# Transposing the second batch's quantised x as pairs of bytes, and loading its ctx with neighbouring rows in a partition

## The chip, the cores and the metric

The kernel runs on one core of one Trainium2 chip. The metric is the time of one execution on the device in microseconds. Before the change it is 1090.87 us, the median of three runs that lie between 1089.13 and 1091.78 us.

## The reference

There are two batches, each with an x of 1024 x 2048 and a ctx of 2048 x 2048, in float32. Two layers follow each other, and each adds to x.

```python
def fake_quant(x, scale, zp):
    q = jnp.clip(jnp.round(x / s + z), 0.0, 255.0)
    return (q - z) * s
...
x = x + jnp.matmul(fake_quant(_layernorm(x)), fake_quant(ctx_4096))
z = _layernorm(x)
x = x + z @ kernel + bias + lora_of_the_group(z) + shared_lora(z)
```

The first layer normalises each row of x, rounds it to whole numbers from 0 to 255, rounds ctx in the same way, and multiplies the two. The second layer multiplies a normalised x with a 2048 x 2048 matrix and adds low-rank terms. Its eight groups of 256 rows have gates of their own.

## The kernel before

The work is cut by batch (b = 0, 1), by group of 256 rows (g = 0 to 3, two tiles of 128 rows each, so a tile has an index m = 0 to 7), and by block of 512 columns (n = 0 to 3).

**x.** A tile's preparation is the class `XTile`. `stats`, `variance`, `root` and `factors` find the mean and the scale (VectorE, but for one square root on ScalarE). `row` writes the 2048 rounded values as bytes into `q8` (in the second batch ScalarE, line 409). `centre` subtracts 128 and writes bfloat16 into `qh`, one half of 1024 columns at a time, and its accumulator gives half of the row's sum (ScalarE, line 412). `turn` transposes that half in eight blocks of 128 x 128 on TensorE into a PSUM tile `pt` (line 423). `place` copies `pt` into the bfloat16 tile `c1T`, with the features on the partitions (line 428, VectorE; for some tiles of the first batch line 427, ScalarE). `total` turns the two half sums into `r_s`, the correction for the zero point (line 432).

**ctx.** Each load from memory (line 213, SyncE's queue) brings 256 rows of 512 columns into one of ten buffers `lit`. `round_ctx` rounds them on ScalarE to int16 (line 458); that frees the buffer, and the next load of the queue can be issued. `centre_ctx` clips and centres them on VectorE into `c2` (line 464). `column_term` sums a block's columns (lines 486 to 511).

**The product.** A `Pair` is one group times one column block: two tiles j, for each of which `begin` (line 526, ScalarE, high priority) writes the corrections into PSUM, and 16 matmuls of 512 columns add to them (line 530). `end` adds the result to `y` (line 547, VectorE), and line 551 takes statistics for the second layer.

**The second layer** is a block matrix product of seven outer steps by seven inner ones (line 829, float32). During the last outer step of the first batch, `meanwhile` already prepares the second batch: after inner step s it rounds two pieces of ctx, and after steps 1 to 4 it prepares the tiles m = 0 to 3. Tiles 4 to 7 are prepared later, between the second batch's products, once `opened`, the first of them, is done.

**What sets the order.** The first batch's first layer follows an order written out by hand (`STEPS`). Everything else is put in order at build time by a list scheduler, which takes for each engine the ready instruction of highest priority, and priority is the order in the program. At run time every engine and every DMA queue works in that fixed order. SyncE's queue holds the loads of ctx, of x (line 226) and of the weights; ScalarE's queue also issues the stores of the finished output (line 855). The x of the second batch goes into the same `y` tiles that hold the first batch's result, so a load of x has to wait for a store; the second halves of the rows of tiles 4 to 7 come last.

Of the kernel before, what the change touches and what calls it, by code (L numbers as in the profile page):

```python
# [11 lines left out]
BF16 = mybir.dt.bfloat16  # L12
U8 = mybir.dt.uint8
I16 = mybir.dt.int16
AF = mybir.ActivationFunctionType
# [5 lines left out]
P = 128  # L21
# [77 lines left out]
def tile_quant_xattn_then_lora_ffn(  # L99
# [17 lines left out]
    nc = tc.nc  # L117
    B, S, D = x.shape
    KT = D // P
    MT = S // P  # L120
    NB = 512
# [9 lines left out]
    KH = KT // 2  # L131
# [8 lines left out]
    ps_m = ctx.enter_context(tc.tile_pool(name="ps_m", bufs=2, space=PSUM))  # L140
# [17 lines left out]
    r_s = const.tile([P, MT], F32, tag="r_s", name="r_s")  # L158
# [13 lines left out]
    def flat(t):  # L172
        return t.rearrange("p k n -> p (k n)")
# [3 lines left out]
    lb = lora_bt.rearrange("(n c r) i -> n c r i", n=NL, c=NC)  # L177

    def raw_src(b, n, r):
        return [ctx_in[b, ds(2 * r * P, 2 * P), ds(n * NB, NB)].rearrange("(k p) n -> p k n", p=P)]  # L180

    def ad_src(t, n, h):

# [4 lines left out]
    for b in range(B):  # L188
        for n in range(2):
            todo.extend((b, raw_src(b, n, r)) for r in range(KT // 2))  # L190
        if b == 0:
            todo.extend((b, m) for m in range(4, MT))
        for n in range(2, 4):
            for r in range(KT // 2):
                todo.append((b, raw_src(b, n, r)))
                if r in ((3, 7) if n == 2 else (5, 7)):
                    todo.extend((b, ad_src(la, 2 * (n - 2) + r // 6 if n == 3 else r // 4, h)) for h in range(2))
        for n in range(NN):
            todo.extend((b, ad_src(lb, n, h)) for h in range(2))
# [79 lines left out]
    s12, d1, d2, kdd = (k_s[:, i : i + 1] for i in range(4))  # L279
    n_centre = const.tile([P, 1], F32, tag="n_centre", name="n_centre")  # L280
# [17 lines left out]
    ident_h = const.tile([P, P], BF16, tag="ident_h", name="ident_h")  # L298
# [67 lines left out]
    class XTile:  # L366


        def __init__(self, b, m, c1T, wk):
            self.b, self.m, self.nm = b, m, f"{b}_{m}"  # L370
            self.on_vector = b == 0 and m not in ROWS_ON_SCALAR
            g, tok = m // MG, ds((m % MG) * P, P)
            self.y = y[g][:, m % MG, :]

            wf = flat(wk)
            self.q8 = wf[:, ds((m % 2) * (D // 4), D // 4)].bitcast(U8)
            self.qh = wf[:, D // 2 : D].bitcast(BF16)
            self.to = [c1T[g][:, ds(h * KH, KH), tok] for h in range(2)]
            self.pt = [None, None]

# [44 lines left out]
        def place(self, h):  # L425
            if self.b == 0 and h == 1 and self.m in PLACED_BY_SCALAR:
                return nc.scalar.copy(self.to[h], self.pt[h])
            return nc.vector.tensor_copy(self.to[h], self.pt[h])  # L428

        def total(self):  # L430

            nc.vector.tensor_scalar(
                r_s[:, self.m : self.m + 1], self.rsum[:, 0:1], self.rsum[:, 1:2], d2, ALU.add, ALU.mult
            )

    def prep_x(b, m, c1T, wk):

        x = XTile(b, m, c1T, wk)
        x.stats(*range(NN))
        with tc.high_priority() if b == 0 else nullcontext():  # L440
            x.variance()
            x.root()
            x.factors()
            x.row()
        for h in range(2):
            x.centre(h)
            x.turn(h)
            x.place(h)
        x.total()

    def quantise(c2, r):
# [569 lines left out]
    for b in range(B):  # L1021
        if b == 0:
            open_c2(0)
            open_c2(1)
            with in_order(mybir.EngineType.DVE, mybir.EngineType.Activation, mybir.EngineType.PE):
                opened, begun = entry()
            next_block(1)
            with tc.issue_after(last_of[mybir.EngineType.DVE]):
                for p in begun.values():
                    p.stats()  # L1030
        else:
            gate_matrix(b)
            opened = xattn_pair(b, 0, 0, c1T, c2[0])
            xattn_pair(b, 0, 1, c1T, c2[0])
            for g in range(2):
                xattn_pair(b, 1, g, c1T, c2[1])
            for g in range(2, GPB):
                for m in range(g * MG, (g + 1) * MG):
                    with tc.issue_after(opened.ins):
                        prep_x(b, m, c1T, wk)  # L1040
                for n in range(2):
                    xattn_pair(b, n, g, c1T, c2[n])
                    if g + 1 == GPB:
                        next_block(n)
                        if n == 0:
                            for r in range(NR):
                                quantise(c2[2], r)
                                if r % 4 == 3:
                                    lora_a_step(b, r // 4)
                            column_term(b, 2, c2[2])  # L1050
# [64 lines left out]
        def meanwhile(o, s):  # L1115
# [27 lines left out]
            if 1 <= s <= 4:  # L1143
                prep_x(nb, s - 1, state["c1T"], state["wk"])
# [77 lines left out]
```

## Time and profile before

| | |
|---|---|
| runs | 1089.13, 1090.87, 1091.78 us |
| span of the profiled execution, first to last instruction | 1086.6 us |
| median less that span | 4.3 us |
| TensorE matmul, busy | 1063.4 us, 98% |
| VectorE, busy | 759.3 us, 70% |
| ScalarE, busy | 247.6 us, 23% |
| DMA, mean rate | 241 GB/s |
| second batch: `row` / `centre` / `place` / transposes | 8 / 16 / 16 / 128 instructions |

A busy share is the union of an engine's instructions over the span. The end of a matmul is modelled, so a busy TensorE need not be one at its peak rate. Times are counted from the start of the span, and no time of the execution that was profiled is given beside its span. The passage that the change touches runs from about 505 us (the last outer step of the first batch's second layer) to about 626 us (the second batch's third column block).

### The profile page before, as it was taken

The page shows a single profiled execution, that of the slowest core. Times are in us where ns is not written, and L with a number is a line of the kernel's source. Part 1 is how long each engine was busy: PE and PEld are TensorE (multiplying, and loading weights), DVE is VectorE, ACT ScalarE, POOL GpSimd, SP SyncE. Part 2 cuts the span into 40 slices and gives each one's busy share as a digit, 9 for nine tenths or more (in the row PEclk, how much of TensorE's full clock was granted, in tenths as well). Part 3 has the DMA queues.
Part 4 walks back from the last instruction along what each step waited for, and adds up shares of the span by engine and source line. Part 5 has one row for each costly group of instructions (what it writes and reads, how often), then busy time and mean ns, then how long its engine had stood idle before and what let it go on. Part 6 is the DMA issues. An engine that isn't in the chain of part 4 may idle for free.

```text
span 1086.6 us, 10640 instructions
## 1 busy us (share of the span) xinstructions
PE 1063.4 (98%) x3932; PEld 491.3 (45%) x3932; DVE 759.3 (70%) x941; ACT 247.6 (23%) x351; POOL 267.8 (25%) x112
## 2 busy tenths in 40 slices
PE   5999999999999999999999999999999999999998
PEld 2444445544444444444444433555444444444443
DVE  7986776756877686677858645757569677756851
ACT  5866133210000000001676631331000000000000
POOL 0000003243434314362000000034344532253500
PEclk7999999999999999999999999999999999999999
DMA  9979758876897575798682394679668874748511
GB/s 344 378 200 295 214 189 327 311 250 218 290 361 271 181 269 182 255 357 300 221 281 49 124 245 164 222 273 349 237 237 292 293 266 154 270 144 301 212 40 58
DMA packets 120380, 261.35 MB, mean 241 GB/s; under 512 B 11400, under 2 KB 15624, under 8 KB 119304
## 3 DMA queue, kind: packets, MB, share of 16 engines
q1 hardware_dynamic: 99840, 219.24, 59.1%
q10 hardware_dynamic: 20168, 40.38, 10.9%
q0 software_dynamic: 320, 1.05, 0.3%
q8 instruction: 31, 0.51, 0.2%
q14 instruction: 21, 0.17, 0.1%
HBM read 224.99 MB, written 37.75 MB: 242 GB/s over the span
## 4 chain that ended last, share of the span: by engine, by line
PE 87%; DVE 5%; DMA 4%; ACT 2%; issue 1%; SPq 0%; ACTq 0%
PE fu L829 34%; PE fv L829 17%; PE pa L530 14%; PE fw L829 9%; DMA lit<-in_ctx_dram 3%; PE pl L695 3%; PE px L649 3%; PE ptz L633 2%; DMA y<-in_x_dram 1%; PE pg_b L576 1%; DVE st L383 1%; PE pg_a L576 1%; ACT big L412 1%; PE pt L423 1%; DVE big L629 1%
## 5 line engine op out<-in xcount | busy, mean ns | idle before, releaser
L829 PE MATMUL fu<-big,lit 128*128 128x512 f32 x896 | 395.3, 593 | 0.0
L829 PEld LDWEIGHTS fu<-big,lit 128*128 128x128 f32 x896 | 168.7, 190 | 206.2 <-issue 204.9
L530 PE MATMUL pa<-big,big 128*128 128x512 bf16 x1024 | 238.8, 381 | 5.0 <-DVE big L428 2.6
L829 PE MATMUL fv<-big,lit 128*128 128x512 f32 x448 | 197.9, 594 | 0.0
L772 POOL TENSOR_TENSOR lit<-lit,lit 128x1024 f32<-128x1024 f32 x56 | 164.2, 2940 | 116.4 <-PE fw L829 49.2
L763 POOL TENSOR_TENSOR lit<-lit,lit 128x1024 f32<-128x1024 f32 x40 | 100.2, 2508 | 289.1 <-DMA lit<-zs 257.7
L772 DVE TENSOR_TENSOR big<-big,big 128x2048 f32<-128x2048 f32 x56 | 159.6, 2853 | 5.9 <-PE ptz L633 5.3
L530 PEld LDWEIGHTS <-big 128*128 128x128 bf16 x1024 | 96.7, 98 | 136.5 <-issue 31.8
L853 DVE TENSOR_TENSOR y<-y,fu 128x1024 f32<-128x1024 f32 x92 | 108.6, 1215 | 50.7 <-PE fu L829 50.5
L829 PEld LDWEIGHTS fv<-big,lit 128*128 128x128 f32 x448 | 84.3, 190 | 105.0 <-issue 104.7
L853 DVE TENSOR_TENSOR y<-y,fv 128x1024 f32<-128x1024 f32 x48 | 56.8, 1218 | 89.4 <-PE fv L829 89.4
L458 ACT ACTIVATE q2b<-lit,sc,inv 128x1024 int16<-128x1024 f32 x64 | 76.3, 1232 | 161.8 <-DMA lit<-in_ctx_dram 126.1
L763 DVE TENSOR_TENSOR big<-big,big 128x2048 f32<-128x2048 f32 x40 | 104.2, 2604 | 11.8 <-DMA big<-in_w_dram 11.8
L829 PE MATMUL fw<-big,lit 128*128 128x512 f32 x224 | 99.6, 593 | 0.0
L680 POOL DMA_DIRECT2D bp<-bd x4 | 2.7, 664 | 376.8 <-DVE rstd_z L358 183.4
L684 ACT COPY pl<-bias 128x1024 f32<-128x1024 f32 x16 | 16.3, 1018 | 294.4 <-DVE y L706 281.4
L547 DVE SCALAR_TENSOR_TENSOR y<-pa,k_s,y 128x1024 f32<-128x1024 f32 x32 | 41.0, 1280 | 47.0 <-PE pa L530 46.8
L829 PEld LDWEIGHTS fw<-big,lit 128*128 128x128 f32 x224 | 41.8, 190 | 51.4 <-issue 50.2
L853 DVE TENSOR_TENSOR y<-y,fw 128x1024 f32<-128x1024 f32 x24 | 28.4, 1216 | 50.9 <-PE fw L829 50.9
L526 ACT ACTIVATE pa<-bp,r_s 128x512 f32<-128x512 f32 x58 | 39.0, 685 | 84.8 <-PE pa L530 54.8
L383 DVE BATCH_NORM_STATS2 st<-y 128x6 f32<-128x512 f32 x64 | 41.4, 680 | 5.4 <-DMA y<-in_x_dram 5.3
L551 DVE BATCH_NORM_STATS2 st<-y 128x6 f32<-128x512 f32 x64 | 40.1, 678 | 0.1
(92 smaller groups left out, 637.3 us busy)
## 6 DMA issues: line engine op xcount, KB each, us to landing
big<-in_w_dram SPq DMA_DIRECT2D x96, 1024.0 KB
lit<-zs SPq DMA_DIRECT2D x88, 512.0 KB
lit<-in_ctx_dram SPq DMA_DIRECT2D x64, 512.0 KB
out_dram<-y ACTq DMA_DIRECT2D x30, 512.0 KB
zs<-lit ACTq DMA_DIRECT2D x24, 512.0 KB
lit<-in_lora_a_dram SPq DMA_DIRECT2D x32, 256.0 KB
lit<-in_lora_bt_dram SPq DMA_DIRECT2D x32, 256.0 KB
y<-in_x_dram SPq DMA_DIRECT2D x16, 512.0 KB
```

Of the source, the lines that this page charges most:

```text
L383: nc.vector.bn_stats(st1[:, self.m, n, :], self.y[:, ds(n * NB, NB)])
L458: nc.scalar.activation(qi, t, AF.Relu, bias=z2, scale=inv2)
L526: nc.scalar.activation(self.pa[:, j, :], colt[self.n], AF.Identity, bias=r_s[:, m : m + 1])
L530: nc.tensor.matmul(self.pa[:, j, :], self.c1T[:, k, ds(j * P, P)], self.c2[k // 8][:, k % 8, :], start=not self.begun[j], stop=(k == KT - ...
L547: return nc.vector.scalar_tensor_tensor(yp, self.pa, s12, yp, ALU.mult, ALU.add)
L551: nc.vector.bn_stats(st2[:, self.g * MG + j, self.n, :], y[self.g][:, j, ds(self.n * NB, NB)])
L649: nc.tensor.matmul(px[i * 2 * R : (i + 1) * 2 * R, :], acat[:, k, ds(3 * pr + i, 2), :].rearrange("p s r -> p (s r)"), zqs[i][k // KQ][:, ...
L695: nc.tensor.matmul(pl[j][i][:, half], axT[rows, pr, ds(j * P, P)], bt[rows, half], start=False, stop=True, skip_group_check=True,)
L763: line(eng.tensor_tensor(got[0], got[0], got[1], ALU.add if terms[1][2] > 0 else ALU.subtract))
L772: line(eng.tensor_tensor(out_t, at[p], at[q], op))
L829: nc.tensor.matmul(ps[m], at[:, k, ds(m * P, P)], bt[:, k, :], start=(opens and k == 0), stop=(ends and k == KQ - 1), skip_group_check=True,)
L853: line(nc.vector.tensor_tensor(yp, yp, whole[chain], op))
```

## The change

For the second batch a tile's bytes are not centred before the transposes. `turn_pairs` reads two neighbouring bytes as one bfloat16 value and transposes the row in eight blocks in place of sixteen. A partition of the PSUM tile then holds two neighbouring features, one in each byte. `place_pairs` reads the bytes out of PSUM with a step of two, subtracts 128 and writes the bfloat16 tiles, in two ScalarE instructions of 1024 elements. `sum_row` runs once more over the 2048 bytes on ScalarE, for the row's sum alone; what else it writes to `qh` is not read. `total` multiplies that one sum. Since features 2p and 2p+1 of each 256 now stand in partition p, the ctx of the second batch is loaded so that rows 2p and 2p+1 stand in partition p. The first batch is untouched.

```diff
     def raw_src(b, n, r):
-        return [ctx_in[b, ds(2 * r * P, 2 * P), ds(n * NB, NB)].rearrange("(k p) n -> p k n", p=P)]
+        rows = "(k p) n -> p k n" if b == 0 else "(p k) n -> p k n"
+        return [ctx_in[b, ds(2 * r * P, 2 * P), ds(n * NB, NB)].rearrange(rows, p=P)]
...
             self.qh = wf[:, D // 2 : D].bitcast(BF16)
+            self.qh2 = self.qh
...
+        def turn_pairs(self):
+
+            self.pairs = ps_m.tile([P, KT // 2, P], BF16, tag="pm", name=f"pq_{self.nm}")
+            two = self.q8.bitcast(BF16)
+            for r in range(KT // 2):
+                nc.tensor.transpose(self.pairs[:, r, :], two[:, ds(r * P, P)], ident_h)
+
+        def place_pairs(self):
+            bytes_of = self.pairs.rearrange("p r t -> p (r t)").bitcast(U8).rearrange("p (r t e) -> p r e t", e=2, t=P)
+            for h in range(2):
+                nc.scalar.activation(
+                    self.to[h].rearrange("p (r e) t -> p r e t", e=2),
+                    bytes_of[:, ds(h * KH // 2, KH // 2)],
+                    AF.Identity,
+                    bias=n_centre,
+                )
+
+        def sum_row(self):
+
+            nc.scalar.activation(self.qh2, self.q8, AF.Identity, bias=n_centre, accum_out=self.rsum[:, 0:1])
+
         def total(self):
 
+            if self.b:
+                nc.vector.tensor_mul(r_s[:, self.m : self.m + 1], self.rsum[:, 0:1], d2)
+                return
             nc.vector.tensor_scalar(
...
-        for h in range(2):
-            x.centre(h)
-            x.turn(h)
-            x.place(h)
+        x.turn_pairs()
+        x.place_pairs()
+        x.sum_row()
         x.total()
```

## The prediction

> **What bounds the kernel now.** I began with the page's first part and its costliest groups.
>
> ```profile
> PE 1063.4 (98%) x3932; PEld 491.3 (45%) x3932; DVE 759.3 (70%) x941; ACT 247.6 (23%) x351; POOL 267.8 (25%) x112
> ...
> L530 PE MATMUL pa<-big,big 128*128 128x512 bf16 x1024 | 238.8, 381 | 5.0 <-DVE big L428 2.6
> ```
>
> TensorE is busy for 98% of the span, and that is real work: in the chain 16 matmuls of line 530 take 3.56 us, 222 ns each, back to back. A TensorE instruction that disappears is therefore worth its full time, unless the instructions behind it are not ready either. ScalarE's 23% says little, because it is a mean over stages. So I asked for the second batch's preparation by stages. The columns are the stretch in us, its length, the busy us of PE, its weight loads, DVE, ACT and POOL with their counts, then the granted clock, the DMA share and GB/s.
>
> ```profile
> 541.90:564.00 22.10, 21.98 (x119) 9.31 (x118) 10.65 (x27) 19.97 (x22) 0.00 (x0) 1.00 0.77 240
> 564.00:579.80 15.80, 15.80 (x72) 6.95 (x71) 13.91 (x32) 4.24 (x8) 0.00 (x0) 1.00 0.77 231
> 579.80:609.80 30.00, 28.92 (x177) 14.03 (x175) 20.90 (x49) 22.69 (x30) 0.00 (x0) 1.00 0.00 1
> ```
>
> In the first stretch (tiles 2 and 3, and ctx of the second column block) ScalarE has 2.1 us left of 22.1, in the third (tiles 4 to 7) it works 22.7 us of 30, and in between, 4.2 of 15.8. The ordered chain of waits over this passage shows what ends last:
>
> ```profile
> 560.26 1.23 ACT q2b L458
> 561.51 0.44 DVE big L464
> ...
> 561.98 8.89 DMA y<-in_x_dram
> ...
> 579.79 2.10 ACT big L409
> ...
> 584.34 0.62 PE pt L423 x8
> ...
> 595.75 2.08 ACT big L409
> 597.83 2.26 ACT big L412 x4
> 600.09 0.62 ACT pa L526
> ...
> 600.75 3.61 PE pa L530 x16
> ```
>
> Read downwards: a rounding of ctx on ScalarE ends at 561.49 and frees a buffer; the ctx load that waited for it is issued; behind that load in SyncE's queue stand the last two x loads, which go out at 561.98 and land 8.9 us later; VectorE then needs 8.9 us for statistics and factors (it is busy for 13.9 of these 15.8 us), and tile 4's `row` starts at 579.79. From there ScalarE sets the pace. Yet TensorE has nearly always something to do: it idles 1.03 us between 580 and 590, and 4 us in the whole of 500 to 720. So this passage stands on an edge: TensorE is full, and ScalarE is late by hardly anything.
>
> The prices are in the groups by shape (out <- in, count | busy us, mean ns), first of 505 to 705 us, then ScalarE's of the whole span, for a copy that the first batch makes:
>
> ```profile
> L412 ACT ACTIVATE big<-big,n_centre 128x1024 bf16<-128x1024 uint8 x16 | 18.2, 1137 | 1.6 <-PE pt L423 1.5
> L409 ACT ACTIVATE big<-y,ox,kx 128x2048 uint8<-128x2048 f32 x8 | 16.6, 2084 | 2.8 <-DVE ox L402 2.8
> ...
> L428 DVE COPY big<-pt 128x1024 bf16<-128x1024 bf16 x16 | 10.5, 681 | 0.1
> ...
> L423 PE MATMUL pt<-ident_h,big 128*128 128x128 bf16 x128 | 9.5, 219 | 2.1 <-ACT big L412 2.1
> ```
>
> ```profile
> L427 ACT COPY big<-pt 128x1024 bf16<-128x1024 bf16 x6 | 6.0, 1005 | 0.8 <-PE pt L423 0.8
> ```
>
> **The change part by part.**
>
> TensorE: 64 of 128 transposes go. Eight in a row take 0.45 us in the chain, so 64 are 3.6 us, 1.8 of them during the second layer (tiles 0 to 3) and 1.8 between the products (tiles 4 to 7). All of it lies on a full TensorE. Its waits for `centre`, 2.1 us in all (1.09 at 528, twice 0.51 at 583 and 584), become one wait per tile for `row`. Between nothing and 2.1 us is won there; I take 1.0, the two at tile 4, since the wait at 528 is a difference between planned and real time that can come back elsewhere.
>
> VectorE: 16 copies of 0.68 us go, 10.9 us. Only where VectorE is on the path would that count, and in the stretch from 564 to 579.8, where it is, there is no copy. I take nothing for it. `total` is one [128 x 1] operation as before.
>
> ScalarE, per tile. Before: `row` and two `centre`, 4.4 us from one tile's start to its end (548.49 to 552.98). After: `row` 2.08; `sum_row`, 2048 bytes: from the rows of 1024 and 2048 elements each further element costs 0.93 ns, so 1.14 + 0.95 = 2.09, plus 0.1 for reading the accumulator; and two unpackings. No row of the trace reads bytes with a step of two out of PSUM. The nearest are line 427 (same size, out of PSUM, 1.005) and line 412 (bytes, with the bias, 1.137). I take 1.1, less the 0.09 by which neighbours overlap; if a stepped byte counted as two elements it would be 2.08, the far end. Together 6.3 us, 1.9 more per tile and 15 us over eight.
>
> [...]
>
> The added wait: an unpacking stands in ScalarE's queue and waits for transposes, where VectorE's copy did. Behind it are the next `row`, the ctx roundings (line 458), `begin` (line 526) and the output stores (line 855). `sum_row` needs only `row`; a list scheduler will most likely put it into that gap, ahead of the unpacking. A tile is then ready 1.9 us later, and `begin`, which needs the sum, hardly later.
>
> ScalarE's 1.9 us by stage. Tiles 0 and 1 (525 to 541): 3.8 us, which the idle 5.0 us before 541.87 hides; without that gap they would add to the next. Tiles 2 and 3: 3.8 us against 2.1 us of idle, and work that starts at most 1.8 us sooner as the second layer ends sooner. So the sixth rounding of ctx, which lets the x loads out, comes between 1.8 us sooner and 3.8 us later; I take 1.0 later, for the idle time lies in four pieces and not all can be used. The x loads, VectorE's 8.9 us and tile 4's `row` follow: 580.8.
>
> Tiles 4 to 7, from the start of `row` 4: before, tile 5's products started 13.1 us later (592.9), tile 7's 30.0 us later (609.8). After: two tiles of 6.3 and three `begin` of 0.62 give 14.5, less half an unpacking, as the first eight matmuls need only that: about 14. Tile 7: four tiles and eight `begin`, 25.2 + 5.0 = 30.2. TensorE has two pairs between the two, 14.2 us, with 0.9 of transposes and 1.0 of loaded products (line 576), and does not take longer. So the 1.8 us of transposes saved here and the 1.0 of waiting are spent on ScalarE. Those two matmuls of line 576, at 608.8 before, may then stand behind tile 7's start and not in a wait: nothing to 1.0, I take 1.0.
>
> ctx rows: the loads keep 256 pieces of 2 KB; only their order changes. The trace has no such load. Mixed stretches with other layouts ran at 335 to 369 GB/s (558 to 570), so I allow 5% either way, 0.5 us on a landing of 9.7, and take nothing; ten buffers loaded ahead hide it, and without them half a microsecond would reach the third block.
>
> Sum: 1.0 later at tile 4, 0.2 in its pace, 1.0 behind it: +2.2 us. From there to the end all is bound to the products' end (the buffers of the third block are those of the first), so it stays. Against the profiled span of 1086.6 that gives 1088.8. What lies around the span is 4.3 us, median less span, so the forecast is 1093.1; its own range, by the bounds above, is 1090 to 1096.5.
>
> **The rivals.** *ScalarE is hidden, and TensorE's saving counts.* If the ctx roundings or the x loads are put ahead of tile 3's sum and unpacking, `row` 4 starts with the second layer's end, 1.8 us sooner or more, and the 3.6 us of transposes and the 2.1 us of waits are won: 1090.9 - 5.7 = 1085.2. For it: VectorE is lighter, and ScalarE idles 11.6 us of 15.8 just before tile 4. Against it: 19.97 of 22.10 busy before. It decides at a tile 4 that starts before 578.
>
> *ScalarE's queue holds the x loads.* Everything of tiles 2 and 3 plus a wait for transposes inside ScalarE's queue (each up to 1.1 us, as at 528) stands ahead of the store at 555.23 or of the sixth rounding: 3.8 + 2 x 1.1 = 6.0 later, and 1.2 behind it: +7.2, 1098.1. For it: the chain above runs through that rounding, and three queues pass it on. Against it: VectorE and SyncE each have slack there. It decides from 3 us of delay at the last x loads.
>
> *Bytes out of PSUM cost double.* 16 x 1.0 us more on ScalarE, 4.0 of it in tiles 4 to 7 and 2.0 to 4.0 before: +9, about 1100. The only sign is that no row shows the form.
>
> **How the numbers follow.** What a measurement of this kernel can tell from no change is about 0.3%, 3.3 us. The forecast (ScalarE spends what TensorE saves) gets 0.52: 0.31 of it within 0.3%, 0.21 slower, as its range passes 1094.1. The hidden ScalarE gets 0.24, of which 0.22 faster and 0.02 within. The held x loads get 0.17 and the double bytes 0.07, of which 0.01 within and 0.23 slower. So 0.22 faster, 0.34 the same, 0.44 slower. The range of 8 in 10 reaches to the first rival's 1085 and nearly to the last one's: 1085.0 to 1099.5.
>
> **What would show it.** Right: line 423 gone from the second batch but for 64 transposes of 0.056 us; unpackings of 1.0 to 1.15 us, `sum_row` of 2.1; ScalarE's busy time up by 15 us; `row` 4 near 581; TensorE's idle time up by some 3 us between 575 and 612, waiting for line 526 or for the unpacking. Wrong: `row` 4 before 578 or after 584; an unpacking beyond 1.3 us; a time that comes or goes before 505 or after 630; or roundings and x loads in another order around the second layer's end, since that order is the scheduler's and I could only guess it.

## The result, and the profile after

The changed kernel takes 1093.36 us (median; 1090.43 to 1098.56), the kernel before 1088.52 beside it (1086.89 to 1091.78). The ratio is 1.0046, with a 95% interval of 1.003 to 1.0062: slower by about 4.8 us, and by more than the 0.3% that a measurement can tell from no change. The forecast was 1093.1.

The profiled execution has a span of 1094.9 us, 8.3 above that of before. 3.5 of these come late, from a wait for weights: their load is issued at 718 us, VectorE makes an operand of them, TensorE's `fw` (line 854, 829 before) waits 2.08 us for it, and its first ten matmuls then take 6.25 us in place of 4.50, at a granted clock of 0.50. The first line is of the changed kernel, the second of the one before:

```profile
730.22 6.25 PE L854 MATMUL fw<-big,lit 128*128 128x512 f32 x10 [2.08 <-DVE big L788]
```

```profile
723.40 4.50 PE L829 MATMUL fw<-big,lit 128*128 128x512 f32 x10
```

Kernels with the old orders show the same wait in some profiles (`rows_only`, `before_begin_first` below) and kernels with the new ones do not show it in others, so I leave it out; the readings below stop at the first `px` matmul of the second batch (line 674; 705.00 us before, 709.82 after: 4.82 us apart). How often this wait comes in either kernel is not known, and so its share of the 4.8 us is not known either. It is hardly all of them, for the fastest executions of the two kernels are 3.5 us apart as well.

In the changed kernel `row` is line 411, the transposes 437, the unpacking 442, the row sum 451, the ctx rounding 483, `begin` 551, the products 555. First the page (busy us, share, count), then the groups by shape of 505 to 712 us:

```profile
PE 1064.4 (97%) x3868; PEld 489.5 (45%) x3868; DVE 752.0 (69%) x925; ACT 261.0 (24%) x351; POOL 263.8 (24%) x112
...
L555 PE MATMUL pa<-big,big 128*128 128x512 bf16 x1024 | 241.3, 385 | 11.1 <-ACT pa L551 7.3
```

```profile
L442 ACT ACTIVATE big<-pq,n_centre 128x1024 bf16<-128x1024 uint8 x16 | 16.9, 1102 | 2.4 <-PE pq L437 2.4
...
L451 ACT ACTIVATE big<-big,n_centre 128x2048 bf16<-128x2048 uint8 x8 | 16.0, 1998 | 0.0
...
L451 ACT ACTIVATION_READ_ACCUMULATOR big<-big,n_centre 128x1 f32 x8 | 1.5, 191 | 0.0
```

An unpacking takes 1.102 us and a row sum 1.998: the two prices that no row of before showed. ScalarE has 13.4 us more to do. The products' idle time has gone from 5.0 to 11.1 us, 7.3 of it released by `begin`. The third stage, in the columns used before the change, and two stretches of 2 us:

```profile
579.80:609.80 30.00, 25.96 (x130) 11.85 (x129) 14.20 (x39) 28.16 (x28) 0.00 (x0) 0.89 0.00 1
...
584.00:586.00 2.00, 1.08 (x3) 0.40 (x3) 1.33 (x9) 2.00 (x5) 0.00 (x0) 0.50 0.00 0
586.00:588.00 2.00, 2.00 (x6) 0.73 (x5) 0.00 (x0) 2.00 (x3) 0.00 (x0) 0.50 0.00 0
```

In the third stage TensorE is busy 2.96 us less than the 28.92 of before, and ScalarE works 28.2 us of 30. The granted clock, 1.00 in all three stages before, is 0.89; it is 0.50 from 584 to 591, as the short stretches begin to show. TensorE's timeline (start, us; in brackets the idle time before the first of a group, and what ended it) and the ordered chain:

```profile
582.22 0.62 PE L437 MATMUL pq<-ident_h,big 128*128 128x128 bf16 x8 [0.69 <-ACT big L411]
584.92 8.23 PE L555 MATMUL pa<-big,big 128*128 128x512 bf16 x24 [2.08 <-ACT pa L551]
...
593.43 5.34 PE L555 MATMUL pa<-big,big 128*128 128x512 bf16 x24
```

```profile
565.50 8.37 DMA y<-in_x_dram
...
580.07 2.10 ACT big L411
...
582.19 2.09 ACT big L451 x2
584.29 0.59 ACT pa L551
...
584.92 8.23 PE pa L555 x24
```

TensorE's products stop at 581.53, eight transposes follow tile 4's `row`, and then it waits for a `begin` that stands in ScalarE's queue behind tile 4's `row` and row sum. That `begin`, the second of block 1, group 1, runs at 584.20 in both kernels, and the products go on at 584.92 in both. TensorE's timeline before:

```profile
584.34 0.62 PE L423 MATMUL pt<-ident_h,big 128*128 128x128 bf16 x8 [0.51 <-ACT big L412]
584.92 4.48 PE L530 MATMUL pa<-big,big 128*128 128x512 bf16 x20
```

Only, the products now stop 1.2 us sooner (581.53 against 582.70), and 8 transposes in place of 16 fill the time. TensorE stands still for 3.39 us but for these, and then 24 matmuls take 8.23 us; the next 24 take 5.34.

One more wait came that the profile of before does not have. ScalarE's timeline in the third block:

```profile
634.37 1.24 ACT L483 ACTIVATE q2b<-lit,sc,inv 128x1024 int16<-128x1024 f32 x1 [2.14 <-DMA lit<-in_ctx_dram]
635.52 0.67 ACT L551 ACTIVATE pa<-bp,r_s 128x512 f32<-128x512 f32 x1
```

A rounding waits for its ctx load, and the `begin` behind it lets TensorE wait 2.33 us at 636.24. TensorE's timeline, two lines of the changed kernel and one of before:

```profile
622.86 0.38 PE L555 MATMUL pa<-big,big 128*128 128x512 bf16 x1 [0.78 <-ACT pa L551]
...
636.24 4.04 PE L555 MATMUL pa<-big,big 128*128 128x512 bf16 x18 [2.33 <-ACT pa L551]
```

```profile
620.29 0.38 PE L530 MATMUL pa<-big,big 128*128 128x512 bf16 x1 [0.78 <-ACT pa L526]
```

At the first matmul of the second block's last tile the changed kernel is 2.57 us behind (622.86 against 620.29); at `px`, behind this wait, it is 4.82.

### The profile page after: what moved, and what is told of

It reads as the page before. It is cut to its first block, busy times and chain, and to the rows that moved or that the text cites. A ratio compares the mean times of both kernels' runs of the same rounds, so it can differ in the third digit from the quotient of the medians.

```text
span 1094.9 us, 10488 instructions
## 1 busy us (share of the span) xinstructions
PE 1064.4 (97%) x3868; PEld 489.5 (45%) x3868; DVE 752.0 (69%) x925; ACT 261.0 (24%) x351; POOL 263.8 (24%) x112
## 4 chain that ended last, share of the span: by engine, by line
PE 86%; DMA 5%; DVE 5%; ACT 2%; issue 1%; SPq 0%; ACTq 0%; DVEq 0%
PE fu L854 33%; PE fv L854 17%; PE pa L555 15%; PE fw L854 9%; PE pl L720 3%; PE px L674 3%; PE ptz L658 2%; DMA lit<-in_ctx_dram 2%; DMA lit<-in_lora_a_dram 1%; PE pg_b L601 1%; DMA y<-in_x_dram 1%; PE pg_a L601 1%; DVE st L385 1%; DMA big<-in_w_dram 1%; ACT big L451 1%
## 5 line engine op out<-in xcount | busy, mean ns | idle before, releaser
L555 PE MATMUL pa<-big,big 128*128 128x512 bf16 x1024 | 241.3, 385 | 11.1 <-ACT pa L551 7.3
L797 POOL TENSOR_TENSOR lit<-lit,lit 128x1024 f32<-128x1024 f32 x56 | 162.1, 2903 | 119.2 <-PE fw L854 46.9
L788 POOL TENSOR_TENSOR lit<-lit,lit 128x1024 f32<-128x1024 f32 x40 | 98.1, 2454 | 294.2 <-DMA lit<-zs 255.0
L797 DVE TENSOR_TENSOR big<-big,big 128x2048 f32<-128x2048 f32 x56 | 163.0, 2914 | 5.9 <-PE ptz L658 5.3
L788 DVE TENSOR_TENSOR big<-big,big 128x2048 f32<-128x2048 f32 x40 | 105.5, 2637 | 12.9 <-DMA big<-in_w_dram 12.9
L385 DVE BATCH_NORM_STATS2 st<-y 128x6 f32<-128x512 f32 x64 | 41.3, 682 | 6.5 <-DMA y<-in_x_dram 6.4
L489 DVE TENSOR_SCALAR big<-q2b 128x1024 bf16<-128x1024 int16 x64 | 27.6, 440 | 21.4 <-ACT q2b L483 18.4
```

What stands on the lines that cost most here:

```text
L385: nc.vector.bn_stats(st1[:, self.m, n, :], self.y[:, ds(n * NB, NB)])
L489: nc.vector.tensor_scalar(c2[r // 4][:, ds(2 * (r % 4), 2), :], qi, QMAX, CENTRE, ALU.min, ALU.subtract)
L555: nc.tensor.matmul(self.pa[:, j, :], self.c1T[:, k, ds(j * P, P)], self.c2[k // 8][:, k % 8, :], start=not self.begun[j], stop=(k == KT - ...
L788: line(eng.tensor_tensor(got[0], got[0], got[1], ALU.add if terms[1][2] > 0 else ALU.subtract))
L797: line(eng.tensor_tensor(out_t, at[p], at[q], op))
```

## The experiments

Theory A: the loss arises at tile 4, from the gap before 585 us and the clock behind it. Theory B: it is ScalarE's pace. Where an expectation means something else by a letter, it says so. "px" is the first `px` matmul against the 705.00 us of before.

| kernel | row 4 | gap before 586, transposes in it | clock behind | px | ratio to before, interval |
|---|---|---|---|---|---|
| changed | 580.07 | 3.39, 8 | 0.50 | +4.82 | 1.0046, 1.003 to 1.0062 |
| rows_only | 579.27 | | 1.00 | +0.60 | 1.0008, 0.9996 to 1.0019 |
| early_tiles | 581.18 | 4.30, 8 | 0.50 | +3.93 | 1.0023, 1.0009 to 1.0037 |
| late_tiles | 580.47 | 2.98, 8 | 0.50 | +1.68 | 1.0023, 1.0003 to 1.0043 |
| fill_gap | 579.39 | filled | 1.00 | +0.64 | 1.001, 1.0 to 1.0021 |
| after_begin_first | 582.35 | 3.95, 16 (at 590) | 1.00 | -0.27 | 1.0007, 0.999 to 1.0023 |
| before_begin_first | 584.39 | 5.50, 32 (at 594) | 1.00 | +4.82 | 1.0041, 1.0023 to 1.0058 |
| begin_mid | 579.02 | 2.97, 8 (at 589) | 0.50 | +0.85 | 1.0004, 0.9991 to 1.0017 |
| sum_vector | 579.44 | | 1.00 | -0.11 | 0.999, 0.9971 to 1.001 |
| sum_in_row | 576.74 | | 1.00 | -3.47 | 0.998, 0.996 to 0.9999 |
| fill_transposes | 579.81 | 3.47, 31 | 1.00 | +3.23 | 1.0043, 1.0025 to 1.0061 |
| after_third | 579.87 | 3.15, 8 | 1.00 | +0.54 | 1.0026, 1.0008 to 1.0044 |
| fill_transposes_third | 580.67 | 3.28, 31 | 1.00 | +2.12 | 1.0015, 0.9999 to 1.003 |

The gap is the time from the end of one product to the start of the next. px comes from one profiled execution each, the ratio from repeated runs; the two need not agree.

**rows_only**: the kernel before with the loads' row order alone.

```diff
-        return [ctx_in[b, ds(2 * r * P, 2 * P), ds(n * NB, NB)].rearrange("(k p) n -> p k n", p=P)]
+        rows = "(k p) n -> p k n" if b == 0 else "(p k) n -> p k n"
+        return [ctx_in[b, ds(2 * r * P, 2 * P), ds(n * NB, NB)].rearrange(rows, p=P)]
```

> The kernel before with the new row order of the second batch's ctx loads alone; its contraction then meets rows of ctx in another order than features of x. Every engine's and queue's order is that of before, so it isolates the loads. Theory A (ScalarE's added work makes begin and the tiles late, and a gap in TensorE's work lowers its clock): no difference, within 0.1% of before; the landing times of the ctx loads as before. Rival B (the loads themselves are slower, and the third column block waits for them): most of the 4.8 us, 2 to 5 us slower than before, with waits for ctx between 620 and 640 us.

1089.36 against 1088.32 us: no difference that can be told, so the loads' order is not where the loss is.

**early_tiles and late_tiles**: the new path for tiles 0 to 3 alone (m < 4), and for tiles 4 to 7 alone (m >= 4).

```diff
-        x.turn_pairs()
-        x.place_pairs()
-        x.sum_row()
+        if m < 4:
+            x.turn_pairs()
+            x.place_pairs()
+            x.sum_row()
+        else:
+            for h in range(2):
+                x.centre(h)
+                x.turn(h)
+                x.place(h)
```

(`total` takes its branch by the same condition.)

> The changed kernel with tiles 4 to 7 prepared in the old way (their features then don't meet the rows of ctx that belong to them). Theory A: tiles 0 to 3 are prepared under the second layer, where ScalarE has room; they save 1.8 us of transposes, and the gap before 585 us does not grow much: 0 to 2 us faster than before. Rival B (loads) or a rival C (ScalarE's work on tiles 2 and 3 holds back the x loads): 2 to 5 us slower than before, row 4 later than 581.

> The changed kernel with tiles 0 to 3 prepared in the old way (their features then don't meet the rows of ctx that belong to them). Theory A: the loss is here, 3 to 6 us slower than before, with a granted clock of 0.5 for some us around 585 and waits for begin behind a row sum. Rival C: no slower than before, as ScalarE's queue around the second layer's end is that of before.

1091.6 and 1090.09 against 1088.32 us. Each half loses by itself, and neither is the one that gains. Both expectations of theory A missed: the early tiles came as rival C had it (3.3 us slower, the x loads out at 566.22, `row` 4 at 581.18), and the late ones lost 1.8 us, with the halved clock, in place of 3 to 6. With the early tiles alone TensorE reaches tile 4 sooner, and the time goes into a longer wait, before the first transposes:

```profile
584.60 0.62 PE L425 MATMUL pt<-ident_h,big 128*128 128x128 bf16 x8 [3.72 <-ACT big L414]
```

**fill_gap**: nine idle matmuls behind tile 4's transposes, seven of which fall into the gap; all other orders as in the changed kernel (`last` is the last of those transposes).

```diff
...
+            if self.m == 4:
+                with tc.issue_after(last.ins):
+                    junk = ps_m.tile([P, NB], F32, tag="pm", name=f"junk_{self.nm}")
+                    for _ in range(9):
+                        nc.tensor.matmul(junk, zeros_h, ones_h[:, 0:1].to_broadcast([P, NB]), start=True, stop=True)
```

> The changed kernel with nine matmuls of 512 columns into an unused PSUM tile, put behind tile 4's transposes; all else stays in its order, and seven of the nine fall into TensorE's 2.08 us wait before 584.92. Theory A with the clock: the granted clock stays at 1.0 after that wait, the 24 matmuls that took 8.23 us take 5.3, and the kernel is 2 to 3 us faster than the changed one, some 1 to 3 us slower than before, although it does more work. Without the clock (the gap is only a wait for begin): the same as the changed kernel, or slower by up to the 0.4 us of the two matmuls that fall elsewhere.

1090.48 against 1088.32 us, though TensorE does more work. Its timeline and its third stage:

```profile
582.00 1.69 PE L442 MATMUL junk<-ones_h,zeros_h 128*128 128x512 bf16 x7
584.24 3.61 PE L560 MATMUL pa<-big,big 128*128 128x512 bf16 x16 [0.56 <-ACT pa L556]
```

```profile
579.80:609.80 30.00, 27.35 (x147) 12.56 (x144) 13.93 (x34) 28.75 (x29) 0.00 (x0) 1.00 0.00 1
```

The time between the products is hardly shorter (2.90 us), but the clock stays at 1.00. I first took this for the whole answer. But ScalarE's rounding waited only 0.30 us for its load in this profile, so the second wait was missing as well.

**after_begin_first, before_begin_first**: in the changed kernel and in the one before, an edge that puts tile 4's `row` behind the `begin` that TensorE waited for (`opening` holds every `begin` by b, n, g and j).

```diff
-            x.row()
+            with tc.issue_after(opening[b, 1, 1, MG - 1].ins) if b and m == 4 else nullcontext():
+                x.row()
```

> The changed kernel with one edge more: tile 4's row on ScalarE (L411) is queued behind the second begin of the pair of block 1 and group 1, so that this begin does not stand behind a row and a row sum. Theory A (the loss is the wait of TensorE for that begin near 585 us and the halved clock behind it): the begin runs by 580 instead of 584.2, TensorE waits less than 1 us between 581 and 586, the granted clock stays at 1.00 through 609.8, and the time falls by 2.5 to 4.5 us to 1088.5 to 1091. Theory B (the loss is the pace of ScalarE, which has 2 us more to do for a tile, wherever that begin stands): the clock may recover, but tiles 5 to 7 come as late as in the changed kernel (tile 7's products after 612), and the time stays at 1092 to 1094.5.

> The kernel before with the same edge, as the control: its waits at that place are 0.51 and 0.51 us and its clock is 1.00 there. Theory A: at most those 1.0 us are to be had, 1087 to 1089.5 (kernel before 1088.5). Theory B: no difference, 1087.5 to 1089.5. A gain of 3 us or more would say that the edge is worth something of its own, and not a repair of what the change did.

1090.18 and 1094.24 against 1089.29 us: the same edge repairs the changed kernel and costs the other one 4.5 us by the ratio. The second I had not expected. ScalarE's timelines, first of the changed kernel with the edge, then of the one before with it:

```profile
581.72 0.69 ACT L553 ACTIVATE pa<-bp,r_s 128x512 f32<-128x512 f32 x1 [2.92 <-PE pa L557]
582.35 4.06 ACT L411 ACTIVATE big<-y,ox,kx 128x2048 uint8<-128x2048 f32 x2
```

```profile
583.76 0.69 ACT L528 ACTIVATE pa<-bp,r_s 128x512 f32<-128x512 f32 x1 [4.89 <-PE pa L532]
584.39 4.07 ACT L409 ACTIVATE big<-y,ox,kx 128x2048 uint8<-128x2048 f32 x2
```

This corrects my reading. The `begin` cannot run while ScalarE idles before 580: it waits for the products of the pair's first tile. These end at 581.5 in the changed kernel and at 583.7 here. So the edge delays `row` by 2.3 us in the one and by 4.6 in the other (579.79 to 584.39), and there the whole delay reaches px. The wait at 590 in the changed kernel's version, 2.94 us behind the row sum, left the clock at 1.00. My expectation of a begin by 580 was wrong.

**begin_mid**: only the row sum of tile 4 goes behind that `begin`.

```diff
-        x.sum_row()
+        with tc.issue_after(opening[b, 1, 1, MG - 1].ins) if m == 4 else nullcontext():
+            x.sum_row()
```

> The changed kernel with one edge: tile 4's row sum (L451) is queued on ScalarE behind the second begin of block 1, group 1; the row itself stays ahead of it. That begin can go when the products of the pair's first tile are done, near 581.5. Theory A: it runs at 582.2, right behind the row, the wait of 2.08 us is under 0.5 and row 4 is not delayed; but the sum, and with it the first begin of the next pair, comes 2 us later, so that TensorE waits near 587 to 590 for 2 to 3 us instead. With the clock at 1.00 through that wait 1089 to 1091.5; if the clock halves behind the new wait 1092.5 to 1095. Theory B (the pace of ScalarE alone): 1092.5 to 1095 with the clock at 1.00.

1089.55 against 1087.93 us. The wait moved to 586 to 589, as expected, and the clock halved behind it, for 3.4 us (589.44 to 592.85) where the changed kernel has 6.8, and yet the loss was gone; for a halved clock I had expected 1092.5 to 1095. So a halved clock alone does not make the 4.8 us. In the order built here, and in that of after_begin_first, the ctx load for which the changed kernel's rounding waits near 634 also goes out ahead of one of the two pairs of lora_a loads that stand before it otherwise, and neither profile has the second wait.

**sum_vector, sum_in_row**: the third pass of ScalarE goes to VectorE, or away.

```diff
-            nc.scalar.activation(self.qh2, self.q8, AF.Identity, bias=n_centre, accum_out=self.rsum[:, 0:1])
+            nc.vector.tensor_reduce(self.rsum[:, 0:1], self.q8, AX.X, ALU.add)
```

```diff
-                nc.scalar.activation(self.q8, self.y, AF.Identity, bias=self.o, scale=self.k)
+                nc.scalar.activation(
+                    self.q8, self.y, AF.Identity, bias=self.o, scale=self.k, accum_out=self.rsum[:, 0:1]
+                )
...
-        x.sum_row()
         x.total()
```

(In both, `total` also subtracts 128 times 2048.)

> The changed kernel with the row sum of the bytes made by a reduction on VectorE instead of the third pass of ScalarE; in the order that is built, the second begin of block 1, group 1 still stands behind tile 4's row, but no row sum is between them. ScalarE is about 16 us below the changed kernel. Theory A: the begin runs near 582.5, TensorE waits under 1 us, the clock stays at 1.00, 1088.5 to 1091.5. Theory B: ScalarE does less than in the kernel before, so the 3.2 us of TensorE that the change removes come back as a gain: 1084.5 to 1087.5. If VectorE is what is short, its reductions of some 2 us delay the factors of the next tile and the time stays above 1092.

> The changed kernel without the row sum's pass: the sum is accumulated by the row itself, over the values before they are rounded to bytes (that part of the computation is changed). No engine takes the work over. Theory A: as with the sum on VectorE, the second begin of block 1, group 1 is 2 us earlier, TensorE's wait at that place is under 1 us or its clock stays at 1.00; 1087 to 1090.5. Theory B: 1084.5 to 1087, faster than the kernel before by what TensorE no longer does. If neither clock nor pace of ScalarE is the cause it stays at 1092 to 1095.

1088.4 and 1086.24 against 1089.29 us. Without the pass the loss is gone, and where no other engine takes it over the kernel is faster than the one before, by 0.0001 to 0.004 of the time; on VectorE (a reduction took 2.28 us, of 18.2 in all) no difference can be told. The first time lies between the ranges of the two theories, the second in that of theory B: what TensorE no longer does comes back as a gain where no engine has to make up for the sum. `sum_in_row` sums the values before they are rounded. The row of its ScalarE:

```profile
576.74 2.09 ACT L411 ACTIVATE big<-y,ox,kx 128x2048 uint8<-128x2048 f32 x1 [1.44 <-DVE ox L404]
```

**fill_transposes**: as fill_gap, with idle transposes.

```diff
...
+                    junk = ps_m.tile([P, KT // 2, P], BF16, tag="pm", name=f"junk_{self.nm}")
+                    for i in range(32):
+                        nc.tensor.transpose(junk[:, i % 8, :], ident_h, ident_h)
```

> The changed kernel with 32 idle transposes of 128x128 behind tile 4's transposes (23 of them in the gap near 583 us, about 1.7 us, the length of the 7 idle matmuls of fill_gap; 9 later); every order on the other engines and queues as in the changed kernel. Theory A1 (any work of TensorE in the gap keeps the clock, as the 16 transposes before the wait of after_begin_first suggest): clock 1.00 through 609.8, 1089.5 to 1091.5, as fill_gap. [...] If the clock falls and the time is that of fill_gap all the same, the clock is not what the fill bought.

1093.63 against 1087.93 us: the clock of A1 (1.00 through 609.8), but not its 1089.5 to 1091.5. With the clock at 1.00 through this passage the kernel is as slow as the changed one. The first matmul of the second block's last tile starts at 620.95, only 0.66 us behind that of before; what follows is the second wait again (and the wait for `fw` near 728 us):

```profile
632.78 1.24 ACT L488 ACTIVATE q2b<-lit,sc,inv 128x1024 int16<-128x1024 f32 x1 [2.45 <-DMA lit<-in_ctx_dram]
```

**after_third, fill_transposes_third**: that rounding and the `begin` behind it change places; nothing else moves on any engine.

```diff
-                quantise(c2[3], r)
+                with tc.issue_after(opening[b, 2, 0, MG - 1].ins) if b and r == 6 else nullcontext():
+                    quantise(c2[3], r)
```

> The changed kernel with two neighbours on ScalarE exchanged: the seventh ctx round of the fourth block (L483) goes behind the second begin of the third block's first pair (L551) instead of ahead of it; nothing else moves on any engine or queue. In the profiled run of the changed kernel that round waited 2.14 us for its load, and TensorE 2.33 us behind it at 636.24. Theory C (this second wait is the other half of the loss, beside the gap at 585): the wait at 636 is gone, the products of the first pair's second tile start within 0.1 us of the first's end, and the time is 1090.5 to 1092.3. Theory A (the gap at 585 and its clock are all of the loss, the second wait is chance of one profiled run): 1092.5 to 1095.

> fill_transposes with the same exchange. Theory C: with the clock kept at 585 and the second wait (2.64 us in the profile of fill_transposes) gone, nothing of the loss is left but the waits for the begin and the later tiles: 1088.5 to 1091, 2.5 to 5 us under fill_transposes. Theory A: the exchange is worth nothing, 1092.5 to 1095, and why fill_transposes was no faster than the changed kernel at full clock stays open.

1091.62 and 1090.08 against 1088.34 us, both inside the range of theory C. The timelines of after_third, TensorE's and ScalarE's:

```profile
584.72 5.34 PE L556 MATMUL pa<-big,big 128*128 128x512 bf16 x23 [2.08 <-ACT pa L552]
```

```profile
630.58 0.69 ACT L552 ACTIVATE pa<-bp,r_s 128x512 f32<-128x512 f32 x1 [0.20 <-PE pa L556]
631.84 1.24 ACT L483 ACTIVATE q2b<-lit,sc,inv 128x1024 int16<-128x1024 f32 x1 [0.57 <-DMA lit<-in_ctx_dram]
```

The second wait is gone, and the `begin` runs 0.2 us after the products that it waits for. By the ratios the exchange is worth 0.0020 in the one kernel and 0.0028 in the other. From the widths of the intervals each of these is uncertain by 0.0024, so the first alone would not count; both together do. The first timeline brought a surprise: up to this place after_third has the orders of the changed kernel, the same gap but for 0.24 us, and a clock of 1.00. What made the difference was not found.

So the loss has two places in ScalarE's queue, at each of which a `begin` stands behind work that has nothing to do with it: tile 4's `row` and sum near 584, and a rounding that waits for ctx near 634. In the profile of the changed kernel they carry 2.57 and 2.25 us; that sum is near the 4.84 us between the medians, in part by chance, for the execution that was profiled took 1097.87 us. At the first place the standstill itself costs nothing against before, as the products go on at 584.92 in both; what is lost behind it is 1.9 us by the clock, going by after_third (622.86 against 621.00), and 0.7 us that after_third has too. That ScalarE's third pass is the cause is shown by taking it away, which takes the whole loss away. That it acts by these two places is read from the queues and not shown by itself: in sum_in_row `row` 4 also starts 3 us sooner, and in sum_vector VectorE has more to do.

How often the clock halves in an execution without a profile can be read in part from the mean granted clock of each, from which 3.41 us at 0.50, as begin_mid has them, take 0.0016. The mean is 0.995 to 0.998 in 11 of the changed kernel's 12 executions. Of 114 of the kernel before, those that ran beside the experiments, it is so in 18, and 0.999 or 1.000 in 77; the other 19 have 0.994 or less, which can come from the start alone, where the profile of before has 0.50 for 13.7 us. The mean does not tell at which place the clock fell, and the wait for `fw` is one.

Two things stay open. The share of that late wait in the 4.8 us was not told apart. And why the ctx load lands in time in some profiles and 2 us late in others of the same order (0.30 us of wait in fill_gap, 2.45 in fill_transposes) was not found; in rows_only, with all orders of the kernel before, the rounding waited 1.01 us too, so the kernel before is not free of it either. The exchange was not tried on that kernel.

## Why the prediction was right, and where it was not

**The main claim held.** "ScalarE spends what TensorE saves" is what `sum_in_row` shows. Without the third pass `row` 4 starts at 576.74, before the 578 at which the first rival decides, and the time falls below that of before. It falls by 2.2 us by the ratio, and not by the 5.7 of that rival: its 1085.2 lies near the measured 1086.24 because it was counted from 1090.9.

**The prices held.** The unpacking was put at 1.1 us and took 1.102; the row sum at 2.09 and took 1.998; ScalarE's whole at 15 us and came to 13.4. (A tile before, 548.49 to 552.98, is 4.49 us and not 4.4.) Bytes with a step of two out of PSUM cost no more than the plain bytes of line 412 (1.137), and the rival of double cost is gone. The second layer ended 1.7 us sooner (552.26 against 553.93), as the 1.8 us of 32 transposes had it. The loads' row order was worth nothing, as taken.

**Tile 4: right for the wrong reason.** The x loads were taken 1.0 us later, and `row` 4 at 580.8. The loads went out 3.52 us later (565.50 against 561.98), at the far end of the bound, but landed after 8.37 us in place of 8.9, and VectorE needed 6.2 in place of 8.9 us from there: it had done the other statistics meanwhile, in another order. `row` 4 came at 580.07, 0.28 us late. An error of +2.5 us and one of -3.2 cancelled. VectorE's share, taken as nothing, is in the second. The rival of the held x loads has come true by its own sign, 3 us of delay at the last x loads (3.5 and 3.6), but not by its price of 7.2 us at this place; `early_tiles` delays them by 4.2 us and `late_tiles` by 0.6, so it is the work on tiles 0 to 3 that holds them.

**The pace of tile 4 to tile 7: the term that was mis-sized.** 0.2 us was forecast; tile 7's products began 32.3 us after `row` 4 (612.37), 2.3 us more than before. Row sums and `row` were taken as a pace that TensorE shares out evenly. In truth ScalarE's fixed order bunched: the row sums of tiles 5 and 6 and two rows in sequence went ahead of a `begin`, tile 5's products began 20.4 us after `row` 4 and not 14, and TensorE stood before two of the `begin`s. (Tile 5's `begin` of before ends at 593.72, so its products started 14.0 us after `row` 4 there and not 13.1; the 14 that was worked out allowed for no loss at all.) The clock, which the forecast took as 1.00 throughout, then made 24 matmuls 2.9 us longer; against after_third, where it did not fall, it explains 1.9 of the 2.57 us towards the second block's end.

**Behind tile 7.** The 1.0 us for the two matmuls of line 576 did not come: they stand ahead of tile 7's products in both kernels.

**"From there to the end it stays": wrong.** 2.25 us were added in the third block. The prediction knew that the rounding waits for loads and that ten buffers run ahead; it did not ask which `begin` stands behind that rounding. A time that comes after 630 was one of its own signs of being wrong.

**The time was met by luck.** The forecast of 1093.1 met the measured 1093.36 with +2.2 at the products, where 2.57 was read, and with 4.3 us around the span and no later wait, while the median of the kernel before fell from 1090.87 to 1088.52 with more runs. The 4.3 us set a median against the span of another execution; where both are on record for one execution they are 1.7 to 3.1 us apart. Against the new median the step forecast was 2.2 us and the step measured 4.8.

## What to carry to other kernels

When an engine at 98% is relieved, ask not only what its work cost, but in which in-order queue the next release for it stands, and behind what: here a write into PSUM of 0.7 us stood twice behind work of other tiles, and the engine that got there sooner only waited longer. Before and after a repair by an edge, look when the instruction itself could have run: the edge that won 4 us in one order lost 4.5 in another. And one profile that loses a wait proves little where loads vary by 2 us (the rounding waited 0.30 us in fill_gap, 2.45 in fill_transposes); two kernels, each with that one pair of instructions exchanged, told more, and only together.

## What the runs showed of the hardware

In these profiles the length of a standstill does not tell by itself which clock follows. Standstills are counted from the end of the last matmul that is no transpose to the start of the next:

| kernel | standstill, from to us | its length | transposes in it | granted clock |
|---|---|---|---|---|
| early_tiles | 580.88 585.18 | 4.30 | 8 | 0.50 from 585.8 to 589.2 |
| changed | 581.53 584.92 | 3.39 | 8 | 0.50 from 584.0 to 590.8 |
| after_third | 581.57 584.72 | 3.15 | 8 | 1.00 |
| late_tiles | 582.34 585.32 | 2.98 | 8 | 0.50 from 586.2 to 589.6 |
| begin_mid | 585.99 588.96 | 2.97 | 8 | 0.50 from 589.4 to 592.9 |
| after_third | 595.76 598.63 | 2.87 | 8 | 1.00 |
| fill_transposes, second wait | 632.00 634.65 | 2.65 | none | 1.00 |
| changed, second wait | 633.91 636.24 | 2.33 | none | 1.00 |
| changed, `fw` | 728.14 730.22 | 2.08 | none | 0.50 from 730.8 to 734.2 |

(Where the clock changes is worked out from its means over stretches of 1 or 2 us.) The stretches at 0.50 in the table last about 3.4 us and, in the changed kernel at tile 4, 6.8. Behind the same wait of 2.08 us for `fw` the first ten matmuls took 6.25 us in four profiles (the changed kernel, rows_only, sum_vector, fill_transposes) and 4.56 in before_begin_first. What decides between the two clocks no run shows.

With more transposes in them the standstills were followed by 1.00 each time: 3.95 us with 16 (after_begin_first), 3.28 and 3.47 us with 31 (fill_transposes_third, fill_transposes), and 5.50 us with 32 (before_begin_first). In the last, from 588.11 to 593.61, TensorE had no other work than transposes. Its timeline there, and the stage, at 1.00 throughout:

```profile
589.64 0.62 PE L423 MATMUL pt<-ident_h,big 128*128 128x128 bf16 x8 [1.52 <-ACT big L412]
...
593.03 0.62 PE L423 MATMUL pt<-ident_h,big 128*128 128x128 bf16 x8 [0.51 <-ACT big L412]
```

```profile
579.80:609.80 30.00, 25.95 (x156) 12.88 (x156) 18.25 (x47) 21.57 (x28) 0.00 (x0) 1.00 0.00 1
```
